# A two-layer vision block on one core: three edits to the order of the outlook-attention stage

## The chip, the cores and the metric

The kernel runs on one core of a Trainium2 chip. The metric is the device time of one execution in microseconds (us), as the median of several runs. Beside it there is one execution recorded by the hardware profiler, from which all rows below come. Times in rows are microseconds from the start of the profiled span.

A core has five engines, each working through its own queue in order: TensorE (PE, matrix products, with its weight loads shown as PEld), VectorE (DVE, elementwise work and reductions), ScalarE (ACT, copies and exponentials), GpSimd (POOL) and SyncE (SP). SP does no arithmetic here. It issues transfers (DMAs), which sixteen DMA engines carry out. An engine whose next instruction waits stands still, and everything behind it in its queue stands too.

## The reference

The input is 4 images of 32 x 32 tokens with 384 channels, in single precision. Two layers follow each other, each with an attention and a feed-forward part around residual additions:

```python
x = x + _L0_conv_ref(_ln_c(x), qkv_w, gp_w, proj_w)          # attention with group selection
t = t + _L0_ffn_ref(_ln_t(t), ...)                           # four experts, two per token
x = x + _L1_conv_ref(_ln_c(x), Wv, Wa, Wo)                   # outlook attention
t = t + _L1_ffn_ref(_ln_t(t), ...)                           # weights are Kronecker products
```

The change lies in the third part and in what prepares the fourth. Outlook attention computes, for each token and each of 12 heads, a 9 x 9 table of scores from the token's own normalised channels, takes a softmax over each row of the table, and uses the 9 rows as weights on the 3 x 3 neighbourhood of value vectors. The results of the nine positions are then added back onto the image, shifted:

```python
a = einsum('bhwc,oc->bhwo', x, Wa).reshape(b, n, heads, 9, 9)
attn = softmax(a * d ** (-0.5), axis=-1)
out = einsum('bnhpq,bnqhd->bnphd', attn, v_unf)              # v_unf: the 3 x 3 patches of x @ Wv.T
for p, (i, j) in enumerate(nine shifts):
    canvas[:, i:i + h, j:j + w] += out[:, :, :, p]
y = canvas[:, 1:h + 1, 1:w + 1] @ Wo.T
```

## The kernel before, in words

The tokens are cut into 32 tiles of 128 tokens (four image rows each), 8 tiles to an image. The function `outlook` runs steps 0 to 36. In step i several tiles are worked on, each at another stage: the scores of tile i, the normalisation of tile i+1, the collection of shifted weights of tile i-2, and the product with the values of tile i-4. The order inside a step is written out by hand, and each engine's queue holds its instructions in the order of the program (the stage is wrapped in a manual schedule). So the place of a line in the step sets what waits behind what.

The pieces of a step, with their lines:

- `sort(i-4)` (ACT, L1991): three copies of the band that has come back from memory into the tile `own`.
- `outer(i-2)` (ACT, L1942 and L1943): two small copies out of the tiles `down` and `up` into `u`.
- `scores(i)`: per half three matmuls of 128x486 (PE, L1881, `ps_a`), then on DVE a maximum and a subtraction (L1887, L1888).
- `exps(i)` (ACT, L1895): the exponential over the whole table.
- `inner(i-2)` (DVE, L1949 to L1951): three additions into `u`; the second and third read `up`.
- `norm(i+1)` (DVE, L147, writes `xn`): the normalised next tile.
- `mix` (PE, L2019, `ps_wo`) and `mixed` (DVE, L2026): the output product of finished tiles. There is none in steps 0 to 8, 16, 24 and 32; two in steps 11, 19, 27 and 35, four in step 36; one in the others from step 9 on.
- `gather(i-4)` (PE, L2004, `ps_y`): the product of `own` with the values, over all heads.
- `turn(i+1)`: three transposes of `xn` (PE, L155, `ps_tr`) and a copy to `xnT` (ACT, L156). The scores of step i+1 read `xnT`.
- `values(i)`: PE L1928 (`ps_v`), ACT L1932.
- `share(i)`: on DVE four additions for the softmax's sums (L1901 to L1905), a reciprocal (L1906) and three multiplications (L1908), then four small transfers on SP (L1918 to L1922) which move the weights by one image row into the tiles `up` and `down` of this and the neighbouring tiles. The first of them, L1918, gives the last rows of `up` of tile i-1. It is left out when i is the first tile of an image.
- `band(i-2)`: three shift matmuls, each in two parts (PE, L1960, `ps_c`), two masked copies (DVE, L1968, `co`), a transfer of `co` to a room in device memory (SP, L1975, 150 KB), and a transfer back of the band (SP, L1981, 1560 KB). The second waits until the first has landed, and SP's queue stands meanwhile.
- `add` (DVE, L1844, L137, L138) and `ask` (POOL, L1541): the experts' results for tiles 17 to 31 are gathered from memory (`yt`) by GpSimd's own queue, for some steps ahead. In the profile the last such gather is at 2468.48 us.

At the start of steps 1, 2, 5 and 8 `loads` issues further input on SP: images of x in the first three (in step 1 the output weights too), and in step 8 `kron.load`, the factors for the last stage. That function issues seven transfers and then places three small DVE operations that read the last two of them (L2127, L2130, L2132). The last stage itself is `kron.run`.

Steps can be found in the profile by the start of their scores: step 3 at 2282.46 us, step 9 at 2371.64 us, step 16 at 2454.35 us.

Of the kernel before, what the change touches and what calls it, by code (L numbers as in the profile page):

```python
# [10 lines left out]
FP = mybir.dt.float32  # L11
# [6 lines left out]
P = 128  # L18
# [3 lines left out]
NT = B * NB  # L22
# [1744 lines left out]
def outlook(net, wv, wa, wo, left, router, kron, loads):  # L1767
# [10 lines left out]
    tc, nc = net.tc, net.nc  # L1778
    K2, H6 = 9, NH // 2
    HW_ = K2 * K2 * H6  # L1780
    PW = K2 * H6
    R = 5 * NH
    with ExitStack() as ctx:
        const = ctx.enter_context(tc.tile_pool(name="ol_const", bufs=1, reuse_waits="tile"))
        work = ctx.enter_context(tc.tile_pool(name="ol_work", bufs=2, reuse_waits="tile"))
# [64 lines left out]
        attn, vs, landed, bands, ys, moved = {}, {}, {}, {}, {}, {}  # L1850
        us, made, xnTs = {}, {}, {}

        def place(i):
            return divmod(i, NB)
# [11 lines left out]
        def norm(i):  # L1866
            xn = work.tile([P, C], FP, name="xn", tag="xn")
            net.ln_apply(xn, i, i, net.mv, net.rs)
            return xn
# [24 lines left out]
            flat = attn[i].rearrange("p y s x e -> p (y s x e)")  # L1894
            nc.scalar.activation(flat, flat, AF.Exp, scale=QK_SCALE)  # L1895

        def share(i):
            b, t = place(i)
            a = attn[i]
            rows = work.tile([P, 2, 3, PW], FP, name="a_rows", tag="a_rows", bufs=1)  # L1900
            nc.vector.tensor_tensor(rows, a[:, 0], a[:, 1], ALU.add)  # L1901
            nc.vector.tensor_tensor(rows, rows, a[:, 2], ALU.add)
            sm = work.tile([P, 2, PW], FP, name="a_sum", tag="a_sum")
            nc.vector.tensor_tensor(sm, rows[:, :, 0, :], rows[:, :, 1, :], ALU.add)
            nc.vector.tensor_tensor(sm, sm, rows[:, :, 2, :], ALU.add)  # L1905
            nc.vector.reciprocal(sm, sm)  # L1906
            for qi in (0, 2, 1):
                nc.vector.tensor_tensor(  # L1908
                    a[:, qi], a[:, qi], sm.unsqueeze(2).to_broadcast([P, 2, 3, PW]), ALU.mult
                )  # L1910
            flat = [a[:, qi].rearrange("p s x e -> p (s x e)") for qi in range(3)]
            if t == 0:
                moved[b, 0] = room(b, 0)
            if t + 1 < NB:
                moved[b, t + 1] = room(b, t + 1)
            down, up = moved[b, t]
            if t:
                nc.sync.dma_start(out=moved[b, t - 1][1][P - IMG :, :], in_=flat[0][:IMG, :])  # L1918
            nc.sync.dma_start(out=up[: P - IMG, :], in_=flat[0][IMG:, :])
            nc.sync.dma_start(out=down[IMG:, :], in_=flat[2][: P - IMG, :])  # L1920
            if t + 1 < NB:
                nc.sync.dma_start(out=moved[b, t + 1][0][:IMG, :], in_=flat[2][P - IMG :, :])  # L1922
# [16 lines left out]
        def outer(i):  # L1939
            u = us[i] = work.tile([P, 6, 5, H3], FP, name="u", tag="u")  # L1940
            down, up = halves(i)
            nc.scalar.copy(u[:, :, 0, :], down[:, :, 0, :])  # L1942
            nc.scalar.copy(u[:, :, 4, :], up[:, :, 2, :])  # L1943
# [81 lines left out]
        def mixed(i, ps):  # L2025
            nc.vector.tensor_tensor(net.x(i), net.x(i), ps[:, :C], ALU.add)  # L2026
# [9 lines left out]
        t_kron, first, gauged = 0, left[0], []  # L2036
        columns()
        turn(0, norm(0))
        for step in range(last + 1):
            i = step  # L2040
            if step in loads:
                loads[step]()
            if 0 <= i - LAG < NT:
                sort(i - LAG)
            if 0 <= i - 2 < NT:
                outer(i - 2)
            if i < NT:
                scores(i, 0)
                scores(i, 1)
                exps(i)  # L2050
            if 0 <= i - 2 < NT:
                inner(i - 2)
            if i + 1 < NT:
                xn = norm(i + 1)
            done = []
            for one in mixes.pop(step, []):
                done.append(mix(*one))
                if len(done) == 2:
                    mixed(*done[0])
                    mixed(*done[1])  # L2060
                    gauged += [j for j, _ in done]
                    done = []
            if 0 <= i - LAG < NT:
                gather(i - LAG, 0 if (i - LAG) % NB < 5 else 1)
            if i + 1 < NT:
                turn(i + 1, xn)
            for one in done:
                mixed(*one)
                gauged.append(one[0])
            if i < NT:  # L2070
                values(i)
                share(i)
            if 0 <= i - 2 < NT:
                band(i - 2)
            if 0 <= i - LAG < NT and (i - LAG) % NB == 4:
                gather(i - LAG - 1, 1)
                gather(i - LAG, 1)
            if coming:
                add()
                if left and left[0] % NB == 0 or not left and not coming:  # L2080
                    until = left[0] if left else NT
                    net.scale(first, until)
                    first = until
            if step >= 3 and left:
                ask(left.pop(0))
            while gauged and gauged[0] < kron.GT:
                kron.gauge(0, gauged.pop(0))
            if step == 2 * NB + LAG + 3:
                kron.begin(0)
            elif step > 2 * NB + LAG + 3 and t_kron < kron.GT:  # L2090
                for _ in range(2):
                    kron.shrink(0, t_kron)
                    t_kron += 1
# [3 lines left out]
class Kron:  # L2097
# [8 lines left out]
    A, K = 32, 12  # L2106
# [10 lines left out]
    def load(self, fc1T, fc2, proj1T, proj2):  # L2117
        nc, A, K = self.nc, self.A, self.K
        const = self.const
        p2 = self.p2  # L2120
        for q in range(4):
            nc.sync.dma_start(out=self.wf[A * q : A * q + A, :], in_=fc1T)
        nc.sync.dma_start(out=self.wp, in_=proj1T.rearrange("(f p) a -> p f a", p=P))
        nc.sync.dma_start(out=self.f2, in_=fc2.rearrange("a b -> (a b)").partition_broadcast(P))
        nc.sync.dma_start(out=p2, in_=proj2.rearrange("a b -> (a b)").partition_broadcast(P))
        self.f2sum = const.tile([P, 1], FP, name="f2sum")
        nc.vector.tensor_reduce(self.f2sum, self.f2, AX.X, ALU.add)  # L2127

        row = const.tile([P, A], FP, name="row")
        nc.vector.tensor_reduce(row, self.net.ident.rearrange("p (q a) -> p a q", a=A), AX.X, ALU.add)  # L2130
        self.wide = const.tile([P, A, K], FP, name="wide")
        nc.vector.tensor_tensor(  # L2132
            self.wide, row.unsqueeze(2).to_broadcast([P, A, K]), p2.unsqueeze(1).to_broadcast([P, A, K]),
            ALU.mult,
        )
        self.xr = [const.tile([P, self.GT, A], FP, name=f"xr_{g}", tag=f"xr_{g}") for g in range(NT // self.GT)]
# [156 lines left out]
def metaformer_kernel(  # L2293
# [19 lines left out]
    def rest(router, done):  # L2313

        with ExitStack() as late:

            pool = late.enter_context(tc.tile_pool(name="late", bufs=1, reuse_waits="tile"))
            kron = Kron(net, late, pool)
            net.xs = {}
            net.home(pool, 0)  # L2320
            wa, wv, wo = (
                pool.tile([P, KC, w.shape[-1]], FP, name=n, tag=n)
                for n, w in (("wa", WaT), ("wv", WvT), ("wo", WoT))
            )
            for b in range(1, B):
                net.home(pool, b)

            def fetch(b):
                first, last = b * NB, (b + 1) * NB
                net.load(x2, range(first, min(last, done)))  # L2330
                net.load(x1, range(max(first, done), last))

            def weigh(queue, tile_, w):
                queue.dma_start(out=tile_, in_=w.rearrange("(k p) o -> p k o", p=P))

            net.load(x2, range(NB), tc.nc.gpsimd)
            weigh(tc.nc.gpsimd, wa, WaT)
            weigh(tc.nc.gpsimd, wv, WvT)
            loads = {
                1: lambda: (fetch(1), weigh(tc.nc.sync, wo, WoT)),  # L2340
                2: lambda: fetch(2),
                5: lambda: fetch(3),
                8: lambda: kron.load(fc1T, fc2, proj1T, proj2),
            }
            eng = mybir.EngineType
            with tc.manual_schedule(engines={eng.PE, eng.DVE, eng.Activation, eng.SP, eng.Pool}):
                outlook(net, wv, wa, wo, range(done, NT), router, kron, loads)
            kron.run(out)

    with ExitStack() as outer:  # L2350
        router = routing(outer)
        eng = mybir.EngineType
        with tc.manual_schedule(engines={eng.PE, eng.DVE, eng.Activation, eng.SP}):
# [3 lines left out]
            done = experts(net, router, x1, x2, wup, wdown, left)  # L2357
# [75 lines left out]
```

## Time and profile before

| what | value |
|---|---|
| median of 3 runs | 2778.15 us (2777.52 to 2788.7) |
| the profiled execution's own time | 2777.38 us |
| its span in the trace | 2774.9 us |
| mean granted TensorE clock | 0.959 |
| outlook steps, first scores to the last stage's first product | 2251.5 to 2686.2 us |
| PE idle in 2245 to 2690 us, put down to `xn` (L147) | 33.5 us in 11 waits, the longest 14.9 us |
| the band's way back (L1981), issues | 32 of 1560 KB |

The timeline of an engine gives start, duration, line, operation, tile written and tiles read, with the idle time ahead of an instruction and what ended it in brackets. Rows marked SPq are the moments at which SP issues a transfer, not the transfer itself; when a transfer has landed is seen from the instruction that waited for it. The chain of waits follows the execution back from its last instruction to whatever released each step, so its rows can be added up.

### The profile page before, as it was taken

Reading aid. Unit: us, or ns where it says so; the run is one execution under the profiler, and the core shown is the slowest. Engines: PE = TensorE matmul, PEld = TensorE weight load, DVE = VectorE, ACT = ScalarE, POOL = GpSimd, SP = SyncE. Lnnn points to the kernel's source line nnn. Section 1 sums busy time; section 2 is a strip of 40 time slices with the busy share of each in tenths; the row PEclk is TensorE's granted clock in tenths of the full one; section 3 lists DMA queues with packets and bytes.
Section 4 is the critical chain, followed back from the end, with each engine's and each line's share of the span. In section 5 each row is a group of like instructions: output and inputs, shape, how many; then the busy total and the mean of one; then the engine's idle time right before and its main releaser. Section 6 shows DMA issues by size and latency. Waiting matters only on the chain. (4 is left out here: it accounts for less than half of the span.)

```text
span 2774.9 us, 40133 instructions
## 1 busy us (share of the span) xinstructions
PE 2565.5 (92%) x14667; PEld 1558.3 (56%) x14667; DVE 1728.3 (62%) x4362; ACT 1301.9 (47%) x2119; POOL 417.8 (15%) x501
## 2 busy tenths in 40 slices
PE   6889999999999998789999999999999987999988
PEld 3323333333333332247889999999999953555532
DVE  1367778677778787647444544465455556887962
ACT  3778777677778777412221221121121123455455
POOL 1000000030003001413211112222222101110000
PEclk9989999999999998889999999999999999999989
DMA  5133434322322232454665545655655447565532
GB/s 108 33 103 92 108 86 126 95 60 63 96 73 64 59 107 69 133 175 160 230 238 207 202 170 216 232 194 217 237 205 211 175 145 221 165 201 175 173 110 93
DMA packets 215806, 404.13 MB, mean 146 GB/s; under 512 B 83344, under 2 KB 176848, under 8 KB 202544
## 3 DMA queue, kind: packets, MB, share of 16 engines
q1 hardware_dynamic: 184496, 187.82, 22.6%
q0 software_dynamic: 26960, 209.05, 22.0%
q10 hardware_dynamic: 4144, 4.61, 0.5%
q8 instruction: 118, 1.93, 0.3%
q14 instruction: 88, 0.72, 0.1%
HBM read 304.34 MB, written 49.00 MB: 127 GB/s over the span
## 5 line engine op out<-in xcount | busy, mean ns | idle before, releaser
L1702 ACT ACTIVATE h<-ps_h,up 128x256 f32<-128x256 f32 (+1 forms) x420 | 195.1, 465 | 825.3 <-PE ps_h L1697 823.7
L1697 PE MATMUL ps_h<-xbT,up 128*128 128x256 f32 (+1 forms) x2520 | 531.1, 371 | 2.5 <-ACT h L1702 1.8
L689 DVE CUSTOM_DVE_ANT_0 e<-e,rz,inv 128x1024 f32<-128x1024 f32 x384 | 475.3, 1274 | 47.3 <-DMA rz<-r_row 47.3
L1697 PEld LDWEIGHTS ps_h<-xbT,up 128*128 128x128 f32 x2520 | 462.6, 191 | 64.6 <-ACT h L1702 2.6
L637 ACT ACTIVATE e<-ps_s,ten 128x1024 f32<-128x1024 f32 x384 | 408.0, 1109 | 66.6 <-PE ps_s L627 40.1
L627 PE MATMUL ps_s<-q,k 32*128 32x512 f32 x1536 | 297.4, 671 | 51.5 <-ACT e L637 35.0
L645 PE MATMUL ps_o<-e,wv 128*32 128x512 f32 x1536 | 227.2, 666 | 40.3 <-DVE wv L696 38.8
L716 POOL DMA_DIRECT2D q<-po x96 | 76.2, 886 | 947.6 <-DMA q<-po 452.9
L645 PE MATMUL ps_z<-e,rt_ones 128*32 128x512 f32 x1536 | 217.1, 639 | 0.0
L373 ACT ACTIVATE below<-tk_left,tk_bound 128x1024 bf16<-128x1024 f32 (+1 forms) x160 | 184.4, 1152 | 52.4 <-DVE tk_bound L379 41.4
L1741 PE MATMUL ps_y<-wsum,hsum 128*128 128x192 f32 x1116 | 196.0, 329 | 9.5 <-DVE hsum L1657 5.2
L627 PEld LDWEIGHTS ps_s<-q,k 32*128 32x128 f32 x1536 | 92.8, 191 | 189.1 <-ACT e L637 92.0
L1741 PEld LDWEIGHTS ps_y<-wsum,hsum 128*128 128x128 f32 x1116 | 182.5, 191 | 13.2 <-DVE hsum L1657 6.6
L1881 PE MATMUL ps_a<-wa,xnT 128*128 128x486 f32 x384 | 162.1, 571 | 0.6 <-ACT xnT L156 0.6
L1745 DVE TENSOR_TENSOR y<-ps_y,y 128x192 f32<-128x192 f32 x155 | 55.5, 358 | 165.5 <-PE ps_y L1741 162.4
L645 PEld LDWEIGHTS ps_o<-e,wv 128*32 128x32 f32 x1536 | 31.5, 112 | 201.0 <-issue 66.1
L288 PE MATMUL ps_t<-xnT,wqkv 128*128 128x512 f32 x288 | 134.6, 607 | 2.4 <-ACT xnT L470 1.7
L1541 POOL DMA_INDIRECT yt<-yg,index x64 | 78.1, 1220 | 375.5 <-DVE x L1844 181.4
L645 PEld LDWEIGHTS ps_z<-e,rt_ones 128*32 128x32 f32 x1536 | 52.2, 117 | 132.0 <-issue 128.8
L1741 PE MATMUL ps_y<-down,h 128*128 128x192 f32 x744 | 126.0, 326 | 0.0
L1741 PEld LDWEIGHTS ps_y<-down,h 128*128 128x128 f32 x744 | 122.6, 190 | 1.6
L1991 ACT COPY own<-band 128x1040 f32<-128x1040 f32 x96 | 101.7, 1125 | 33.2 <-DMA band<-room 30.8
(398 smaller groups left out, 3576.7 us busy)
## 6 DMA issues: line engine op xcount, KB each, us to landing
band<-room SPq DMA_DIRECT2D x32, 1560.0 KB
rz<-r_row SPq DMA_DIRECT2D x48, 512.0 KB
yg<-y SPq DMA_DIRECT2D x67, 192.0 KB
q<-q SPq DMA_DIRECT2D x192, 64.0 KB
k<-k SPq DMA_DIRECT2D x192, 64.0 KB
room<-none SPq DMA_DIRECT2D x64, 192.0 KB
x<-x SPq DMA_DIRECT2D x35, 192.0 KB
o<-in_x_dram SPq DMA_DIRECT2D x33, 192.0 KB
```

The source lines that it names most:

```text
L288: nc.tensor.matmul(ps, lhsT=lhsT(k), rhs=rhs(k), start=k == 0, stop=k == KC - 1)
L373: nc.scalar.activation(junk[:n], left[:n], AF.Sign, bias=bound[:n], accum_out=over[:n])
L627: nc.tensor.matmul(ps[:, half * 512 : half * 512 + 512], lhsT=self.k4[r, u * P : (u + 1) * P], rhs=self.q4[r, :], start=True, stop=True,)
L637: nc.scalar.activation(e, ps, AF.Exp, bias=shift, scale=QK_SCALE)
L645: nc.tensor.matmul(ps[r : r + 32, :], lhsT=lhsT(odd), rhs=self.es[2 * u + odd][:, half * 512 : half * 512 + 512], start=u == 0, stop=u == ...
L689: nc.vector.tensor_tensor_reduce(self.es[m], self.es[m], self.rz, 1.0, self.im["inv"][:, m, self.h : self.h + 1], ALU.mult, ALU.add, self. ...
L1541: self.nc.gpsimd.indirect_dma_start(out=y, out_offset=None, in_=self.net.yg[: first_row(self.complete(i // NB)), :], in_offset=bass.Indire ...
L1697: nc.tensor.matmul(ps, lhsT=up[:, o : o + P], rhs=xbT[:, k, :size], start=k == 0, stop=k == KC - 1,)
L1702: nc.scalar.activation(hs[f // 3][:, f % 3, :size], ps, AF.Gelu, bias=up[:, KC * HID + f : KC * HID + f + 1])
L1741: nc.tensor.matmul(ps, lhsT=left[f], rhs=right[:, f, :], start=f == 0, stop=f == HF - 1)
L1881: nc.tensor.matmul(pa[:, :HW_], lhsT=xnTs[i][:, k, :], rhs=wa[:, k, hh * HW_ : (hh + 1) * HW_], start=k == 0, stop=k == KC - 1,)
L1991: nc.scalar.copy(own[:, pairs], m.rearrange("p t (n h) -> p n t h", h=2)[:, pairs])
```

## The change

Three things are moved, and nothing is added to or taken from the arithmetic.

1. `norm(i+1)` stands ahead of `scores(i)` in the step instead of behind `inner(i-2)`.
2. `share` is cut in two. Its four additions become `total(i)`, placed ahead of the band; the reciprocal, the multiplications and the four SP transfers stay where they were. `band(i-2)`, with its PE, DVE and SP parts, moves from the end of the step to a place behind `total(i)` and ahead of `gather(i-4)`. A single `mixed` moves ahead of these too.
3. `kron.load` keeps its seven transfers in step 8. Its three DVE operations become `kron.fold`, placed in step 14.

```diff
-        def share(i):
-            b, t = place(i)
+        def total(i):
             a = attn[i]
...
             nc.vector.tensor_tensor(sm, sm, rows[:, :, 2, :], ALU.add)
+
+        def share(i):
+            b, t = place(i)
+            a, sm = attn[i], sums.pop(i)
             nc.vector.reciprocal(sm, sm)
...
+            if i + 1 < NT:
+                xn = norm(i + 1)
             if i < NT:
                 scores(i, 0)
                 scores(i, 1)
                 exps(i)
             if 0 <= i - 2 < NT:
                 inner(i - 2)
-            if i + 1 < NT:
-                xn = norm(i + 1)
...
+            for one in done:
+                mixed(*one)
+                gauged.append(one[0])
+            if i < NT:
+                total(i)
+            if 0 <= i - 2 < NT:
+                band(i - 2)
             if 0 <= i - LAG < NT:
                 gather(i - LAG, 0 if (i - LAG) % NB < 5 else 1)
             if i + 1 < NT:
                 turn(i + 1, xn)
-            for one in done:
-                mixed(*one)
-                gauged.append(one[0])
             if i < NT:
                 values(i)
                 share(i)
-            if 0 <= i - 2 < NT:
-                band(i - 2)
...
+    def fold(self):
+        nc, A, K = self.nc, self.A, self.K
+        const, p2 = self.const, self.p2
         self.f2sum = const.tile([P, 1], FP, name="f2sum")
         nc.vector.tensor_reduce(self.f2sum, self.f2, AX.X, ALU.add)
...
                 8: lambda: kron.load(fc1T, fc2, proj1T, proj2),
+                14: kron.fold,
```

In the changed program PE's queue in a step reads scores, output product, shift, gather, transposes, values. SP's queue reads room and band of tile i-2, then the four small transfers of tile i; before it was the small transfers first.

More of the change, by code (lines that the diff above doesn't have):

```diff
@@ L1895, in exps @@
             nc.scalar.activation(flat, flat, AF.Exp, scale=QK_SCALE)
-        def share(i):
-            b, t = place(i)
+        sums = {}
+        def total(i):
             a = attn[i]
@@ L1902, in share @@
             nc.vector.tensor_tensor(rows, rows, a[:, 2], ALU.add)
-            sm = work.tile([P, 2, PW], FP, name="a_sum", tag="a_sum")
+            sm = sums[i] = work.tile([P, 2, PW], FP, name="a_sum", tag="a_sum")
             nc.vector.tensor_tensor(sm, rows[:, :, 0, :], rows[:, :, 1, :], ALU.add)
             nc.vector.tensor_tensor(sm, sm, rows[:, :, 2, :], ALU.add)
+        def share(i):
+            b, t = place(i)
+            a, sm = attn[i], sums.pop(i)
             nc.vector.reciprocal(sm, sm)
```

## The prediction

> **What bounds the kernel now.** I read the page's first part, then the timeline of each engine over the outlook stage (2250 to 2686 us), since only this stage changes, and last PE's waits and the chain of waits.
>
> ```profile
> PE 2565.5 (92%) x14667; PEld 1558.3 (56%) x14667; DVE 1728.3 (62%) x4362; ACT 1301.9 (47%) x2119; POOL 417.8 (15%) x501
> ```
>
> PE is busy 92% of the whole span, which says nothing of this stage. A late step (step 18) on PE:
>
> ```profile
> 2478.60 5.05 PE L1881 MATMUL ps_a<-wa,xnT 128*128 128x486 f32 x12
> 2483.49 2.10 PE L2019 MATMUL ps_wo<-wo,y 128*128 128x384 f32 x6
> 2485.52 1.60 PE L2004 MATMUL ps_y<-own,v 128*32 128x260 f32 x24
> 2487.05 0.55 PE L155 MATMUL ps_tr<-ident,xn 128*128 128x128 f32 x3
> 2487.43 2.10 PE L1928 MATMUL ps_v<-wv,xnT 128*128 128x384 f32 x6
> 2489.37 0.47 PE L1960 MATMUL ps_c<-u,shift 128*128 128x180 f32 x2
> ```
>
> No brackets: PE never waits, and the next scores start at 2490.28, 11.7 us on. From step 9 PE alone sets the pace, but for 2.10 us each in steps 16 and 24. In steps 0 to 8 it waits for `xn` nearly every time, longest in step 8, where DVE stands for a factor of the last stage (rows of PE, of DVE, and of PE's waits):
>
> ```profile
> 2364.15 0.87 PE L155 MATMUL ps_tr<-ident,xn 128*128 128x128 f32 x3 [14.89 <-DVE xn L147]
> ```
> ```profile
> 2359.39 0.17 DVE L2127 TENSOR_REDUCE f2sum<-f 128x1 f32<-128x12 f32 x1 [12.96 <-DMA f<-in_fc_dram]
> ```
> ```profile
> PE ps_tr L155 <- DVE xn L147: 33.5, 11, 14.9
> ```
>
> The change removes these waits (the 0.93 for tile 0 stays): up to 32.6 us. The question is what is late next.
>
> **What is late next: the small transfers.** In SP's queue L1918 to L1922 of tile i now stand behind the band of tile i-2, whose issue waits for the room to land. Step 7 of before shows an `up` piece (L1918) issued 2.1 us behind a band (SP, ACT, DVE):
>
> ```profile
> 2326.42 0.34 SPq L1981 DMA_DIRECT2D band<-room  x1
> 2328.54 0.54 SPq L1918 DMA_DIRECT2D up<-attn  x1
> ```
> ```profile
> 2335.11 3.15 ACT L1991 COPY own<-band 128x1040 f32<-128x1040 f32 x3 [6.93 <-DMA band<-room]
> ```
> ```profile
> 2335.33 0.27 DVE L1950 TENSOR_TENSOR u<-attn,up 128x108 f32<-128x108 f32 x1 [0.17 <-DMA up<-attn]
> ```
>
> The small piece landed 0.2 us after the big one. In step 2, with the queue nearly free, it took 1.9 us (issue 2271.53, its reader at 2273.47). So a piece behind a band comes when the band is done.
>
> The price by rows: ACT's copy of `up` (L1943) stands ahead of the exponential in ACT's queue, the exponential ahead of `total`, `total` ahead of `co`, and `co` ahead of the next room. That closes a ring from one step's `up` to the next one's. Its links, of ACT, DVE and the chain of waits:
>
> ```profile
> 2324.22 0.28 ACT L1943 COPY u<-up 128x108 f32<-128x108 f32 x1 [2.37 <-DMA up<-attn]
> 2324.41 1.01 ACT L1895 ACTIVATE attn<-attn 128x972 f32<-128x972 f32 x1
> ```
> ```profile
> 2325.45 0.50 DVE L1901 TENSOR_TENSOR a_rows<-attn 128x324 f32<-128x324 f32 x1 [0.39 <-ACT attn L1895]
> ```
> ```profile
> 2658.73 6.65 DMA band<-room
> ...
> 2666.38 6.20 DMA band<-room
> ```
>
> `up` landed to `total`: 1.23 (2324.22 to 2325.45). `total`: 1.67 (its four additions, to the reciprocal at 2327.12). `co` to the room's issue: 0.56 (2653.70 to 2654.26). Room issue to band issue: 2.55 (2.42 to 2.71 from step 18 to 31 of before). Band issue to landed: 6.6 (6.20 to 6.77 where its reader waited and no gathers ran). `up` behind it: 0.2. Sum **12.8 us a step**. PE's own step becomes 11.9: the 11.7, and 0.26 because the shift matmuls now follow the output product (1.94 us after the scores) while `u` is ready 2.2 us after them (2376.80 to 2378.84, and 0.15 to PE). So the ring is slower by 0.9 us, and it decides.
>
> Up to step 16 GpSimd's gathers run beside the band. Their price is open: nothing, or 2.1 us (the 8.7 us of the band above, with gathers beside it, against 6.6). The DMA share in 12 us stretches is 0.65 with them and 0.53 without, 1.4 us of all engines. I take 1.2 near that row: 14.0 us a step.
>
> By the Trainium skill, "DMA: Bandwidth & Descriptors", section "Queues, rings and completion order", a later transfer on one queue may complete before an earlier one. That speaks for the change: with it the ring would vanish and the sum would be that of the first rival below. The rows of step 7 speak against it here.
>
> **The sum.** S is the end of a step's scores.
>
> (a) Steps 0 to 8, including the removed stall. In steps 0 and 1 the next scores can start at once behind the copy of `xnT` (2259.58 in place of 2260.84): -1.2 each. Then the ring starts. S(2) is 2272.7 (before 2275.17); `co` ends 4.7 later (exponential 2.45 after S, 1.67, 0.56); room 2.55, and 1.5 for the load of x issued ahead of it (0 to 4.9: in step 5 of before a room behind a load took 7.4), band and `up` 6.8: 2288.2. One link of 12.8, four of 14.0, and 1.5 again for the load in step 5 give 2358.5 for the `up` that step 8 needs. To the scores of step 9: 0.6 to the shift, then 0.92, gather 0.5, transposes 0.4, values 1.94, two gathers 1.5, and 1.5 for a lowered clock: 2365.9, against 2371.64: **-5.7**. The three DVE operations moved to step 14 cost 1.0 us once, hidden in the ring's slack on DVE; uncovered, 1.0. `norm`, moved ahead of the maximum, takes 0.48 of DVE there, while DVE waited 0.45 to 1.9 us for the scores in steps 10 to 18: nothing, or 0.5 a step if the ring leaves DVE late. POOL's queue keeps its order; its gathers wait for `add`, which still follows `share`.
>
> (b) S(9) to S(17), 2376.80 to 2471.98, 95.2 before. Tile 8 begins an image and has no L1918, so step 9 does not wait: 4.7 + 2.55 + 6.8 + 1.2 = 15.25 to the next `up`. Six links of 14.0 are 84.0, 0.7 for step 11, where two output products delay `total`, then 0.6 + 5.3 as above + 4.9 scores = 10.8, and 1.5 for the clock: 112.3. **+17.1**.
>
> (c) S(17) to S(25), 96.9 before (to 2568.88): the same without gathers, 14.05 + 76.9 + 0.7 + 10.8 + 1.5 = 103.9. **+7.0**.
>
> (d) S(25) to S(31), 71.3 before (to 2640.18): 14.05 + 4 x 12.8 + 0.7 + 10.0 (from the last `up` over shift, gather 1.2, transposes, values and scores) = 75.9. **+4.6**.
>
> (e) The tail from S(31) to the last band, 32.4 before (to 2672.58): the last `up` but one 2.8 after S, one link 12.8, then 18.4: additions, shift and `co` 2.0, room 2.5, band 6.5, the last room 1.0 behind it, band 6.4. 34.0. **+1.6**.
>
> Total +24.6. On the profiled execution's 2777.38 that is **2802 us**. This execution lies 0.8 below the median of the runs shown, less than the sum's accuracy.
>
> The 1.5 for the clock comes from these rows: after a gap of 2.59 us the granted clock was 0.67 (2277.7 to 2282.4) and `ps_v` took 3.28 in place of 2.10; after 2.10 us it was 0.66 once (2558 to 2562) and 1.00 once (2462 to 2465.3). I take it in steps 8, 16 and 24, and inside the ring it is hidden. The Trainium skill, "TensorE: Matmul & The Clock Gate", section "Part 1: The HAM clock gate", lowers the clock only after some 3.4 us idle. By that the sum would lose these 4.5 us; the rows show it lowered after less.
>
> **Rivals.**
>
> *The ring does not close (not slower).* If an `up` lands within 5.5 us of its issue although a band is ahead, it meets its reader (issue at S + 4.7 + 2.55 + 0.35 = S + 7.6; needed 1.2 after the next step's scores, ahead of the exponential, thus at S + 13.1). Then PE sets the pace: -3 in steps 0 to 2; steps 3 to 8 take 6 x 11.9 + 4 for clock and loads = 75.5 in place of 89.2, -13.7; 18 steps with one output product lose 0.3 each, +5.4. Sum -11.3: **2766**. For it: step 2's 1.9 us; against it: step 7, and step 6, where an `up` issued at 2316.48 behind a band and a load landed only at 2324.2.
>
> *The ring is there but short.* With 12.3 a link and gathers at 0.3, 22 links lose 0.5 and some 11 lose 0.9 more: -21, **2781**, the stall's removal paying for almost all. For it: the 6.20 row; against it: 6.63 to 6.77 elsewhere.
>
> *The clock stays low.* PE now idles ahead of the shift in every step, 1 to 2 us. Should that lower the clock in ten more steps, 1.5 each: **2817**. Against it: waits of 1.42 and 1.94 (steps 4 and 6) were followed by `ps_v` at 2.10.
>
> That the fold in step 14 still waits for its factors is excluded: they landed 9.4 us after their issue.
>
> **Chances.** Forecast 0.50, short ring 0.20, ring not closed 0.22, low clock 0.08. The range 2764 to 2818 takes in the rivals, and links longer by 0.5. About 0.5% (13.9 us) is what a measurement can tell from no change. Slower by more: the forecast, the low clock and a little of the short ring, 0.60. Faster: less than half of the ring not closed, and hardly anything else, 0.10. Within: 0.30.
>
> **What would show it.** Step 8's wait for `f` is gone, and the scores of step 9 start near 2366. ACT's L1948 (was L1943) waits for `up` in nearly every step but 9, 17 and 25; PE waits ahead of the shift for `u`, no longer for `xn`; steps take 12.8 us after step 18 and 14 before. If L1948 hardly waits and steps take 11.9, the ring is wrong and so is the forecast. If bands take over 8 us throughout, it is too low.

## The result, and the profile after

The changed kernel took **2822.48 us** (median of 4 runs, 2817.16 to 2824.52) against 2780.45 for the kernel before on the same chip: ratio 1.0143, 95% interval 1.0116 to 1.0171. It is slower, by 1.4%. The direction of the forecast holds and its size does not: 2802 was forecast, and the time lies above the range. The profiled execution took 2817.16 us (2777.38 before), so 39.8 us are to be found. From the first scores to the last stage's first product the trace of after has 474.4 us, that of before 434.7: all of it lies in this stage.

The page's first part shows PE 13 us busier, not faster (share of the whole span):

```profile
PE 2578.5 (92%) x14667; PEld 1563.6 (56%) x14667; DVE 1727.7 (61%) x4362; ACT 1300.6 (46%) x2119; POOL 418.3 (15%) x501
```

A late step on PE (timeline; step 22). It has the same instructions as step 18 of before, with the shift behind the output product, and a wait for `u` ahead of it:

```profile
2549.53 5.05 PE L1881 MATMUL ps_a<-wa,xnT 128*128 128x486 f32 x12
2554.42 2.10 PE L2024 MATMUL ps_wo<-wo,y 128*128 128x384 f32 x6
2557.82 0.54 PE L1965 MATMUL ps_c<-u,shift 128*128 128x180 f32 x2 [1.30 <-DVE u L1956]
```

The gather, the transposes and the values follow without a gap, and the next scores start at 2562.74, 13.2 us on, where before needed 11.7. The waits over the stage and a little beyond (2250 to 2780 us; total, times, longest) show what took the place of the 33.5 us for `xn`:

```profile
ACT u L1948 <- DMA up<-attn: 94.8, 23, 9.0
ACT u L1948 <- DMA down<-attn: 20.6, 5, 5.7
PE ps_c L1965 <- DVE u L1956: 67.0, 28, 8.9
PE ps_tr L155 <- DVE xn L147: 0.9, 1, 0.9
```

The wait for `xn` is gone but for tile 0, and in step 8 nothing stands for `f` (DVE; the fold now runs in step 14):

```profile
2442.09 0.13 DVE L2138 TENSOR_REDUCE f2sum<-f 128x1 f32<-128x12 f32 x1
```

In its place PE waits for `u`, and `u` for the small transfers. In five links the profile names a `down` piece as what the copy of `up` waited for. The trace also keeps the completion counts of each transfer, which has landed when the last of them comes in. By these the `up` piece came in 0.07 to 0.08 us before the copy in those five links too, and the `down` pieces only after the copy had begun. The page's chain of waits, by engine, has DMA 9% (2% before) and PE 5% (14% before); 6% is `up` and 2% the room:

```profile
DMA 9%; PE 5%; DVE 4%; ACT 1%; issue 0%; SPq 0%; DVEq 0%; ACTq 0%
```

In order of time the same chain shows the ring that the prediction drew, one link (start, length, what; three more additions are left out):

```profile
2557.20 0.28 ACT u L1948
2557.49 0.93 ACT attn L1895
2558.44 0.51 DVE a_rows L1902
...
2560.07 0.46 DVE co L1973 x2
2560.54 2.47 DMA room<-co
2563.03 0.33 SPq L1986
2563.45 7.24 DMA up<-attn
2570.71 0.29 ACT u L1948
```

The copy of `up`, the exponential, the additions, `co`: 3.34 us. The room: 2.5. SP issues the band at 2563.03, and behind it the last rows of `up`, whose copy starts 7.68 us after the band's issue. By the completion counts the band itself had landed after 7.38 us and the piece 0.28 us later. Together 13.5 us, and then the same again. No PE row is in the link.

Stage by stage, from start to start of a step's scores (the last row to the last stage's first product):

| section | before | after | difference | forecast |
|---|---|---|---|---|
| first scores to step 9 | 120.2 | 117.3 | -2.9 | -5.7 |
| step 9 to 17 | 95.2 | 112.7 | +17.5 | +17.1 |
| step 17 to 25 | 96.9 | 106.9 | +10.0 | +7.0 |
| step 25 to 31 | 71.4 | 81.4 | +10.0 | +4.6 |
| step 31 to the end | 51.0 | 56.1 | +5.1 | +1.6 |
| sum | 434.7 | 474.4 | +39.7 | +24.6 |

### The profile page after: what moved, and what is told of

Its sections match the earlier page's. It is cut to its first block, busy times and chain, and to the rows that moved or that the text cites. A ratio compares the mean times of both kernels' runs of the same rounds, so it can differ in the third digit from the quotient of the medians.

```text
span 2814.9 us, 40123 instructions
## 1 busy us (share of the span) xinstructions
PE 2578.5 (92%) x14667; PEld 1563.6 (56%) x14667; DVE 1727.7 (61%) x4362; ACT 1300.6 (46%) x2119; POOL 418.3 (15%) x501
## 5 line engine op out<-in xcount | busy, mean ns | idle before, releaser
L1741 PEld LDWEIGHTS ps_y<-wsum,hsum 128*128 128x128 f32 x1116 | 182.4, 191 | 13.6 <-DVE hsum L1657 7.1
L1881 PEld LDWEIGHTS ps_a<-wa,xnT 128*128 128x128 f32 x384 | 72.3, 189 | 81.2 <-issue 71.1
```

Source lines behind the costliest of these rows:

```text
L1741: nc.tensor.matmul(ps, lhsT=left[f], rhs=right[:, f, :], start=f == 0, stop=f == HF - 1)
L1881: nc.tensor.matmul(pa[:, :HW_], lhsT=xnTs[i][:, k, :], rhs=wa[:, k, hh * HW_ : (hh + 1) * HW_], start=k == 0, stop=k == KC - 1,)
```

## The experiments

Theory: the ring, closed by the place of `up`'s transfer behind the band in SP's queue, costs more than the change removes. Rivals: the shift right behind the scores does the harm (PE stands for `u` whatever the transfers do), or the load of the DMA engines does it, whichever queue issues.

Eleven kernels ran in three groups, each group on one chip with the kernel before beside it. On these chips the stages ahead of outlook take some 40 to 55 us longer than in the table above, so a kernel is compared with before by the ratio within its group (medians of before: 2829.04, 2819.99 and 2821.85 us). "Stage" is the length of the outlook stage in the kernel's own trace, as in the table (434.7 before, 474.4 after). It comes from one execution on that group's chip; the changed kernel itself has 474.4 and 480.8 on two chips, so a difference of a few us in this column says nothing.

| kernel | group | ratio to before | interval | stage, us |
|---|---|---|---|---|
| changed kernel again | 2 | 1.0168 | 1.0148 to 1.0189 | 480.8 |
| band's way back last | 1 | 0.9982 | 0.9968 to 0.9996 | 429.5 |
| fold alone | 1 | 0.9948 | 0.9931 to 0.9966 | 411.2 |
| fold and early norm | 1 | 0.9900 | 0.9874 to 0.9926 | 404.3 |
| early band alone | 1 | 1.0243 | 1.0213 to 1.0273 | 502.2 |
| way back on GpSimd's queue | 2 | 0.9978 | 0.9962 to 0.9994 | 430.2 |
| the same, SP held back | 3 | 0.9995 | 0.9979 to 1.0011 | 430.2 |
| one piece ahead | 3 | 0.9969 | 0.9956 to 0.9983 | 425.5 |
| three quarters ahead | 3 | 1.0047 | 1.0028 to 1.0065 | 440.8 |
| `up`'s rows last | 2 | 1.0252 | 1.0225 to 1.0280 | 501.0 |
| shift behind the gather | 2 | 0.9908 | 0.9883 to 0.9932 | 403.2 |

### What each part is worth

**Fold alone**: the kernel before, with the three DVE operations in step 14.

```diff
                 8: lambda: kron.load(fc1T, fc2, proj1T, proj2),
+                14: kron.fold,
```

> The kernel before with the last of the three edits alone: the factors' three DVE operations in step 14. Both theories: only step 8's wait of 14.9 us goes, with about 2 for the lowered clock behind it, and 0 to 3 come back because transfers that the stall let catch up are late: 2762 to 2768 us. If the stall was hiding a lateness of the transfers altogether, it stays at 2775 to 2780.

Measured: 2811.49 against 2829.04 us, -17.6, near the upper end of what was expected (12 to 18 below the 2780). PE's waits for `xn` in the first nine steps fall from 28.4 to 13.6 us; the wait of 14.9 has gone and nothing took its place.

**Fold and early norm**: the same, with `norm(i+1)` ahead of the scores.

```diff
+            if i + 1 < NT:
+                xn = norm(i + 1)
             if i < NT:
                 scores(i, 0)
```

> The kernel before with two edits: the next tile normalised ahead of the scores, and the factors in two parts; total and band stay at their old places. Ring theory: the ring needs the early band, so it is absent; the waits for xn (33.5 us with step 8) go, some 5 us of lowered clock with them, and the steps 4 to 8 become bound by DVE at 10.4 us: 2742 to 2758 us. Order theory says the same here, since the shift matmuls stay last in the step. A loss against the kernel before would refute both and put the blame on the early normalisation.

Measured: 2798.96 us, -30.1 against before and -12.5 against the fold alone. So two of the change's three parts remove what the prediction said they could (up to 32.6), and with them the third must cost over 70 us.

**Early band alone**: the changed kernel with norm and fold in their old places.

```diff
                 inner(i - 2)
+            if i + 1 < NT:
+                xn = norm(i + 1)
...
-                8: lambda: kron.load(fc1T, fc2, proj1T, proj2),
-                14: kron.fold,
+                8: lambda: (kron.load(fc1T, fc2, proj1T, proj2), kron.fold()),
```

> The changed kernel without its two other edits: total and band early, the normalisation behind the additions into u and the factors in step 8, as before. Ring theory: the ring runs at the same 13.4 to 14 us a step, and the wait for the factor in step 8 is added to it nearly whole (8 to 15 us), while the place of the normalisation matters by under 4 us, since PE waits for u anyway: 2826 to 2840 us. If the early normalisation is what makes DVE late, the time falls below that of the changed kernel: under 2815.

Measured: 2897.90 against 2829.04, +68.9, more than expected (46 to 60). By the ratios (1.0243 against 1.0143 and 1.0168 of the changed kernel) norm and fold are worth 21 to 28 us here, somewhat less than the 30 without the early band. The waits (2250 to 2790 us) show PE for `u` and hardly for `xn`. The longest, 14.1 us, is step 8, where DVE again stands 12.5 us for the factor `f`; that step takes 26.2 us against 14.9. On DVE (step 22) `xn`, 0.47 us, now stands between `u` and the additions:

```profile
PE ps_c L1965 <- DVE u L1956: 83.7, 31, 14.1
PE ps_tr L155 <- DVE xn L147: 4.8, 3, 1.9
```
```profile
2632.05 0.47 DVE L147 TENSOR_SCALAR xn<-x,mv_x,rs_x 128x384 f32<-128x384 f32 x1
...
2632.90 0.49 DVE L1902 TENSOR_TENSOR a_rows<-attn 128x324 f32<-128x324 f32 x1
```

It takes nothing from the link there: from the copy of `up` to the room 3.35 us pass, as in the changed kernel, where DVE waits 0.30 us for the exponential in this place (step 22). What norm is worth in the ring beside the fold is not settled by this run.

### Is it the ring?

**Band's way back last**: everything of the change stays, but the transfer back (L1986) is issued behind the four small transfers. The shift, `co` and the room stay early.

```diff
-            m = landed[i] = bp.tile([P, BAND, NH], FP, name="band", tag="band", bufs=3)
...
+        def back(i):
+            room = net.room[i % NB]
+            m = landed[i] = bp.tile([P, BAND, NH], FP, name="band", tag="band", bufs=3)
...
                 share(i)
+            if 0 <= i - 2 < NT:
+                back(i - 2)
```

> The changed kernel with one edit: the transfer that brings the band back (1560 KB) is issued behind the four small transfers of the step instead of ahead of them; everything else stays. Ring theory (the small transfers are late because a band stands ahead of them in SP's queue, and ACT, DVE and SP close a ring over them): the ring opens, PE sets the pace with 11.9 us a step, the waits of ACT for up (90 us in the changed kernel) go below 15, and the time falls to 2755 to 2770 us. Rival, order theory (the loss comes from what the move did on PE and DVE: the shift matmuls wait for u right behind the scores, and the clock drops in these gaps): PE's order is untouched, so the time stays above 2805.

Measured: 2823.91 us, ratio 0.9982; the stage takes 429.5 us, 45 to 51 less than after. ACT's wait for `up` falls from 94.8 us to two waits; PE's wait for `u` falls to 29.2, but does not go:

```profile
PE ps_c L1965 <- DVE u L1956: 29.2, 28, 4.6
ACT u L1948 <- DMA up<-attn: 7.5, 2, 5.6
```

The ring is opened by one line's place, and that is worth about 50 us. But only 5 us are won against before, where 10 to 25 were expected and 30 are to be had without the early band. What is left, 25 us, may be the rival's part, the shift right behind the scores; the next kernel tests that.

**Shift behind the gather**: the kernel just shown, with `band` (now shift, `co` and room) moved behind `gather`.

```diff
-            if 0 <= i - 2 < NT:
-                band(i - 2)
             if 0 <= i - LAG < NT:
                 gather(i - LAG, 0 if (i - LAG) % NB < 5 else 1)
+            if 0 <= i - 2 < NT:
+                band(i - 2)
```

> The changed kernel with the way back issued behind the small transfers, and in addition the shift (PE, DVE and the room's transfer) behind the gather in place of ahead of it. If the 25 us by which the kernel with the way back last stays behind the kernel with only the early normalisation and the factors in two parts come from PE's wait for u right behind the scores (29 us in its waits), the wait falls below 8 and the stage from 429.5 to 398 to 406 us. If they come from DVE (the sums ahead of the masked copies), nothing changes: 425 to 432.

Measured: ratio 0.9908, stage 403.2. PE's wait for `u` is 13.7 us in 10 waits, more than the 8 expected, and the time is that of fold and early norm alone:

```profile
PE ps_c L1965 <- DVE u L1956: 13.7, 10, 2.2
```

So both causes are shown: about 50 us for the ring, about 25 for the place of the shift.

**The changed kernel again** ran in group 2, to have the ring's links on that chip.

> The changed kernel itself, unedited, as the measure for the three kernels beside it on the same chip: 1.012 to 1.017 of the kernel before, as first measured, and 474 us from the first scores of the outlook stage to the first product of the last stage. Both theories say the same.

Measured: ratio 1.0168, stage 480.8, 6 us more than on the first chip; the waits are those of after (ACT for `up` 92.1 us, PE for `u` 66.9).

**One piece ahead**: of the four small transfers only the last rows of `up` of tile i-1 (L1923) go ahead of the way back (the diff is against the kernel with the way back last).

```diff
                 nc.sync.dma_start(out=moved[b, t - 1][1][P - IMG :, :], in_=flat[0][:IMG, :])
+            if 0 <= i - 2:
+                back(i - 2)
             nc.sync.dma_start(out=up[: P - IMG, :], in_=flat[0][IMG:, :])
...
                 share(i)
-            if 0 <= i - 2 < NT:
+            elif i - 2 < NT:
                 back(i - 2)
```

> The changed kernel with one small transfer, the last rows of up of tile i-1 (L1923), issued ahead of the band's way back; the other three stay behind it. The ring as I have it runs over this piece alone, because only its reader stands one step later; the other pieces have two steps. So the stage should take 428 to 440 us, as with all four ahead (429.5). The rival, that all four or the down pieces too hold the next step, or that SP's waiting itself does it, leaves 460 us or more, and ACT's waits for down (20.6 us in the changed kernel) should grow.

Measured: ratio 0.9969, stage 425.5, a little under the range. ACT's wait for `up` is down to two waits, and none for `down` is left:

```profile
ACT u L1950 <- DMA up<-attn: 8.1, 2, 6.3
```

The ring runs over this one piece, 32 rows of 324 values or 41 KB, which the next step reads; the others have two steps or more.

### Queue, bytes or engines?

**`up`'s rows last**: the changed kernel with that piece as the last of the four instead of the first.

```diff
-            if t:
-                nc.sync.dma_start(out=moved[b, t - 1][1][P - IMG :, :], in_=flat[0][:IMG, :])
             nc.sync.dma_start(out=up[: P - IMG, :], in_=flat[0][IMG:, :])
...
+            if t:
+                nc.sync.dma_start(out=moved[b, t - 1][1][P - IMG :, :], in_=flat[0][:IMG, :])
```

> The changed kernel with the four small transfers in another order: the last rows of up, on which the next step waits, are issued last in place of first. If the bytes of one queue are moved strictly in the order of issue, up then lands behind 284 KB more, 0.8 to 1 us later in each of some 24 links of the ring: stage 490 to 500 us. If the transfers of one queue run mixed, so that all four land together a good 1 us behind the band's own bytes (which would explain why a link took 13.4 us and not 12.8), the order matters little: 472 to 482.

Measured: stage 501.0 against 480.8, just above the range. From the band's issue to the copy of `up`, the steps without gathers give 8.4 us against 7.6 in the changed kernel on the same chip: 0.8 a link for three small transfers ahead.

**Three quarters ahead**: three quarters of the band's way back in the old place, the last quarter behind the small transfers.

```diff
+            mid = BAND * NH * 3 // 4
+            cut = slice(0, mid) if half == 0 else slice(mid, BAND * NH)
...
-                out=m.rearrange("p t h -> p (t h)"),
-                in_=room[: P * BAND * NH].rearrange("(p r) -> p r", p=P),
+                out=m.rearrange("p t h -> p (t h)")[:, cut],
+                in_=room[: P * BAND * NH].rearrange("(p r) -> p r", p=P)[:, cut],
```

> The changed kernel with the band's way back cut into two transfers: three quarters of each row in the old place, the last quarter behind the four small transfers. If the bytes issued ahead in the same queue set the landing of up, it lands a quarter of 6.4 us earlier, some 6.0 us after the issue of the first part instead of 7.6; the link falls from 13.4 to 11.8 us, which is PE's own pace, and the stage takes 430 to 445 us. If the load of the engines sets it, or a fixed time of waiting, the link stays at 13 or more and the stage takes 465 us or more.

Measured: stage 440.8, inside the range, ratio 1.0047. Two rows of SP, and ACT's copy that waits for the piece:

```profile
2626.99 0.32 SPq L1992 DMA_DIRECT2D band<-room  x1
2627.42 0.54 SPq L1923 DMA_DIRECT2D up<-attn  x1
```
```profile
2633.67 0.28 ACT L1948 COPY u<-up 128x108 f32<-128x108 f32 x1 [3.04 <-DMA up<-attn]
```

Here 6.7 us from the first part's issue to the copy; the mean of the steps without gathers is 6.6. A quarter less (390 KB) is 0.9 to 1.1 us, not the 1.6 that its share of the band's time would be, and the link is 12.3, not 11.8. The bytes ahead in the queue count, but by some 60% of what I had set.

**Way back on GpSimd's queue**: the changed kernel with L1986 on another queue.

```diff
-            nc.sync.dma_start(
+            nc.gpsimd.dma_start(
                 out=m.rearrange("p t h -> p (t h)"),
```

> The changed kernel with one edit: the band's way back is issued by GpSimd's queue in place of SP's, at the same place of the step; the small transfers follow the room directly on SP. Queue theory (a small transfer behind a band on the same queue waits for its bytes): up lands 2 to 4 us after its issue and not 7 to 8, the ring opens, and the stage falls from 474 to about 430 us, as in the kernel with the band's way back issued last (429.5). Rival, engine theory (the sixteen DMA engines are full of the band's bytes, whichever queue they come from): up still lands with the band, and the stage stays above 465.

Measured: ratio 0.9978, stage 430.2, as with the way back last. But this changes two things: SP no longer waits for the room either, so the piece is issued ahead of the band in time: in one step the room at 2606.77, the piece at 2608.07, and the band, on GpSimd's queue, only at 2609.54. So it doesn't tell the queue from the engines. **The same, SP held back** was meant to: a read of 2 KB of the room, which nobody uses, stands at the band's old place on SP, so the piece is issued when it was in the changed kernel.

```diff
+            peek = work.tile([P, 4], FP, name="peek", tag="peek", bufs=2)
+            nc.sync.dma_start(
+                out=peek, in_=room[: P * BAND * NH].rearrange("(p r) -> p r", p=P)[:, :4]
+            )
```

> The changed kernel with the band's way back on GpSimd's queue, as in the earlier kernel of that kind, and in its old place on SP a read of 2 KB of the same room, which nobody uses. SP again waits for the room to land, so the small transfers are issued as late as in the changed kernel, beside or behind the band, but in another queue. If one queue's order delays the last rows of up, they land 2 to 3.5 us after their issue, a ring has some 9 us and does not decide, and the stage takes 428 to 445 us (after 474 to 481). If it is the load of the sixteen DMA engines by the band, whichever queue it came from, they land 6 to 8 us after their issue and the stage takes 465 to 485 us.

Measured: ratio 0.9995, stage 430.2. SP, POOL and ACT of one step:

```profile
2611.17 0.33 SPq L1986 DMA_DIRECT2D peek<-room  x1
2611.60 0.54 SPq L1923 DMA_DIRECT2D up<-attn  x1
```
```profile
2611.71 0.53 POOL L1990 DMA_DIRECT2D band<-room  x1 [10.97 <-DMA room<-co]
```
```profile
2616.29 0.28 ACT L1948 COPY u<-up 128x108 f32<-128x108 f32 x1 [1.39 <-DMA up<-attn]
```

Beside the band, in another queue, the piece takes 4.7 us from its issue (mean of the steps without gathers 4.6). Neither expectation had that: 2 to 3.5 for the queue, 6 to 8 for the engines. The same piece takes 7.1 behind the band in SP's queue, and took 1.9 with a nearly free queue (step 2 of before). With 4.6 the ring is at most 3.4 + 2.5 + 0.4 + 4.6 = 10.9 us, less than PE's step, and doesn't decide.

How much of the 2.5 us between 7.1 and 4.6 is the shared queue is not shown, because the order in time is another one too: here the band is issued 0.1 us after the piece, in the changed kernel 0.4 us before it. In step 11 of this run the piece went out 0.24 us behind the band, still in another queue, and its copy started 6.8 us after its issue (POOL, SP, ACT):

```profile
2425.74 0.58 POOL L1990 DMA_DIRECT2D band<-room  x1 [9.19 <-DMA room<-co]
```
```profile
2425.98 0.54 SPq L1923 DMA_DIRECT2D up<-attn  x1
```
```profile
2432.74 0.28 ACT L1948 COPY u<-up 128x108 f32<-128x108 f32 x1 [1.84 <-DMA up<-attn]
```

In the other steps with gathers where it went out some 0.1 us ahead of the band, it landed after 4.2 to 4.8 us. In step 5, 0.16 us behind it, it took 5.8 us. So a band issued first delays the piece in another queue as well, and these runs do not show what a queue of its own brings at the same order of issue.

## Why the prediction was right in direction and wrong in size

**What bounds the kernel now; what the change removes.** Right. The waits for `xn` went, the three operations in step 14 cost nothing to be seen, and fold and norm alone win 30.1 us.

**What is late next: the ring.** Right, link by link: the chain of after holds exactly the forecast's steps, L1948 waits in nearly every step, and moving one transfer opens it.

**The failed step is a term of the sum: "Band issue to landed: 6.6".** I took 6.6 for the band, from bands that had the queue to themselves, and 0.2 for `up` behind it. The 0.2 held: by the completion counts the piece landed 0.2 to 0.3 us behind the band in every link of after from step 18 on. The band did not: it landed 6.9 to 7.9 us after its issue there (mean 7.3), against 6.1 to 6.7 in the same steps of before, but for one of 7.4. In the ring the four small transfers are issued 0.4 to 2.8 us behind the band. The last two bands of after have none behind them and took 6.5 and 6.2. The other runs with the whole band on SP's queue agree: 6.5 to 6.8 on average where the small transfers are not issued right behind it (before, fold alone, fold and early norm, way back last, shift behind the gather), 7.2 to 7.4 where three or four of them are (one piece ahead, the changed kernel, early band alone, `up`'s rows last). So the missing 0.7 goes with the pieces at the band's back; by what mechanism they slow it is not shown.

The copy of `up` starts 7.5 us after the band's issue in steps 17 to 23 and 7.7 in steps 25 to 30. Summed over the links, the sum's term for this (6.8, 8.0 with gathers, and 1.5 for the load in step 5) is too small by 3.4 us in steps 2 to 7, 0.9 in 9 to 16, 5.2 in 17 to 23, 4.7 in 25 to 29 and 0.7 in the last link. That is 14.9 us, where the whole sum was 15.1 too small; the other errors nearly cancel. Of the other terms, `up` to the room's issue is 3.34 to 3.54 (3.46 forecast) and the room 2.2 to 2.8 (2.55), in the ordinary steps from 18 on.

**Gathers beside the band.** Price forecast 1.2, measured 0.6 to 0.8 (8.1 us in steps 9 to 16 and 8.3 over all steps with gathers, against 7.5). It was too high by nearly as much as the band was too low, so section (b) came out right, 17.5 against 17.1, by two errors.

**Steps with two output products.** I gave 0.7. In step 27, which has two, `up` to the room takes 4.22 us against 3.51 in step 26: the 0.7 holds. But in steps 11, 19 and 24 it takes 4.75 instead of 3.34, and the row is another one (ACT, step 11):

```profile
2403.82 0.28 ACT L1948 COPY u<-up 128x108 f32<-128x108 f32 x1 [2.85 <-DMA up<-attn]
2404.12 1.28 ACT L1895 ACT_TABLE_LOAD   x1
```

Before has the same loads (one at 2401.60), where ACT had time for them. A ring charges for whatever stands in it.

**The first section.** -2.9 against -5.7: the first `up` came as forecast (37 us after the first scores), the links after it were longer by the failed term.

**The tail.** From the end of step 31's scores to the last band 35.9 us, 34.0 forecast. The last link took 13.4 (12.8). Then from `up` to the room 3.4 us where I had 2.0: PE had stood for 8.95 us, and at the clock after it (0.50) the three groups of shift products took 0.94, 0.81 and 0.81 in place of 0.54, 0.47 and 0.47. A further 1.5 us passed behind the last band, which the sum did not reach.

**The clock.** The term holds: after PE's wait of 2.73 us in step 8, `ps_v` took 3.02 in place of 2.10, at a granted clock of 0.78 (2365.8 to 2369.5). The Trainium skill, "TensorE: Matmul & The Clock Gate", section "Part 1: The HAM clock gate", would have it lowered only after some 3.4 us idle; the trace shows it after less, as before did.

**Completion order.** The Trainium skill, "DMA: Bandwidth & Descriptors", section "Queues, rings and completion order", allows a later transfer on a queue to complete first, and that would have opened the ring. No link here shows it: by the completion counts the piece landed 0.2 to 0.9 us behind the band in every link of after.

**The rivals.** "The ring does not close" was refuted, and its price too: with the ring open the kernel wins 1 to 9 us (ratios 0.9969 to 0.9995), where I had 11.3. I had used a step of 11.9 everywhere; but in the steps with no output product the shift has nothing ahead of it but the scores and waits 2.2 us for `u`, and in the others a step of the open kernel takes 12.2, against 11.7 without the early shift. "The ring is there but short" was wrong in sign: it is longer. "The clock stays low" is not seen: after waits of 1.3 us the products run at 2.10.

In sum, by the medians of groups 1 and 2: fold -17.6, early norm -12.5, early shift with an open ring +25.0, the ring +47 to +52 (by the first measurement of the changed kernel and by that of group 2).

**The best version** is fold and early norm, with the band left in its place (ratio 0.9900), or the shift behind the gather with the way back last (0.9908); the intervals overlap. Both beat the kernel before and the changed one.

## What to carry to other kernels

When a large transfer moves ahead of a small one in a queue, look for who reads the small one next: if that reader stands ahead of the next large one, the two close a ring, whose length every step then pays and which no engine's busy share shows. Write the links out and price each by a row in which the same neighbours are present; the row of a band that had the queue to itself was 0.7 us too kind. And try the parts of a combined change one by one: here two were worth 30 us, and the third took over 70.

## What the runs showed of the hardware

- The landing time of a small transfer of 41 KB, from its own issue: 1.9 us alone; 4.6 when a 1560 KB transfer of another queue was issued 0.1 us after it; 5.8 and 6.7 when that was issued 0.16 and 0.24 us before it (one step each, with gathers); 6.1 behind 1170 KB of its own queue; 7.1 behind all 1560 KB of its own queue, 0.4 us after it.
- The 1560 KB transfer itself landed 6.1 to 6.7 us after its issue when it had the queue to itself (late steps of before, but for one of 7.4), and 6.9 to 7.9 with four small transfers issued behind it (after).
- Bytes ahead in the same queue changed a landing by some 2.5 to 3 us per 1000 KB (a quarter of the band: about 1 us for 390 KB; three small transfers: 0.8 for 284 KB), while the band alone took about 4 us per 1000 KB.
- The load of a table on ACT costs 1.28 us each time; in after, three of them stand between `up` and the room (at 2404.12, 2515.64 and 2583.84).
- After 8.95 us without a product (2683.8 to 2692.7) the granted clock was 0.50 in the next 3.3 us and 0.68 in the 4 us after that.
